# Four-column convolutions with six terms, the first one's terms made by TensorE, and new operation tables for two stages of a two-layer kernel

## The chip, the cores and the metric

The kernel runs on one core of one Trainium2 chip, in one launch. The metric is the device time in microseconds (us). The core has a matrix engine (TensorE, PE in the profile, with its weight loads as PEld), a vector engine (VectorE, DVE), a scalar engine (ScalarE, ACT), GpSimd (POOL) and SyncE (SP), which here only issues DMAs. Each engine runs its own instructions in the order in which the program lists them; a wait at the head of an engine's queue holds everything behind it.

## The reference

The input `x` is 16 samples x 128 channels x 32 x 32, all float32. Two layers are applied, each with a mixing part and a feed-forward part, with a residual added after each. Cut to what matters:

```python
# layer 0
x = x + linear_attention(_ln_c(x))        # layer norm over channels, group norm, q/k/v, 4 heads, output projection
t = tokens(x)
t = t + stu(_ln_t(t))                     # long causal convolutions with 16 filters (by transforms), and 3 short taps
x = image(t)
# layer 1
out = conv3x3(_ln_c(x), w1); out = relu(bn1(out))
out = bn2(conv3x3(out, w2)); x = x + relu(out + _ln_c(x))
t = tokens(x)
t = t + routed_experts(_ln_t(t))          # 64 experts, each takes 8 tokens of each sample
return image(t)
```

The two 3x3 convolutions have 128 input and 128 output channels on 32 x 32 images, with a zero border.

## The kernel before, in words

The program is one function with five stages, one after the other.

1. **Attention** (lines 203 to 748). `class Attention` has one method for each operation on one sample: `tokens` transposes the image (8 transposes), `moments`, `variance`, `root` and `scales` make the layer norm's factors, `norm` scales 8 pieces on ACT, then `channels`, `q_`, `k`, the softmaxes, `context`, two folds of the output matrix, `out`, `out_add`, a second norm, and then the transform of the sample by `even` and `odd` (eight residue classes, butterflies on POOL) and the three-tap part (`taps`, line 618, 24 profile records, `taps_add`). The order of the work is written out by hand in the tuple `period`: each entry is an operation and how many samples ahead it runs, up to 6; a loop goes through it once for each sample. The filters' own transform (`filters`) and the mixing of their matrices (`mst`, 16 steps from 16 loads `mi`) and the preparation of weights on POOL (`prepare`) are generators, one step of which is taken per round. Inputs `x0` and `x1` are loaded first, then `wf`, `phi`; `load(b + 2)` stands in `tokens`. PSUM holds three tiles of 1024 columns (`big`).
2. **Transform convolution** (lines 749 to 846): 16 chunks; `generate` makes the matrices of a chunk on TensorE (L776), ACT and DVE copy them out (L785, L783), `multiply` applies them (L796). The change does not touch it.
3. **Layer 1** (lines 847 to 1352). `class Routed` again has a method for each operation on one sample: the inverse transform (`inverse`, L1039, 16 matmuls), the layer norm (`tokens`, `stats`, `copy`, `root`, `scales` on POOL, `norm`), the image, both convolutions, a second norm and the routing (`logits` to `pooled_copy`, once for a pair of samples).
 A convolution makes two columns from four terms: `terms` (L920, DVE) makes four differences and sums of neighbouring columns, `products` (L926) multiplies one pair of terms for one half of the image by the three rows of transformed weights: six matmuls of 256 columns in a PSUM tile `pcv`. `shift` (ACT, L1097), `sums` (DVE, L1105 and L1106) and `rows` (DVE, L1115 and L1116) combine the four products into the two columns; `relu` (ACT, L1119) writes the next input. So there are 2 x 2 x 12 = 48 matmuls for a sample; the profile has two records for a matmul (L926 x1536).
 The order comes from `planned(table, buffers, ...)`: a list scheduler at build time, with the cost, the due time, the dependences and the tiles of each operation in `table`, which plays the operations through and returns a fixed order. The number after the cost is only a priority.
4. **Experts** (lines 1353 to 1448): 32 weight blocks of 1 MB pass through a ring of nine tiles (`RING`, `load_half`).
5. **Output** (lines 1449 to the end of the function): gates times expert outputs, added to `x` and stored.

The lines of `products` that the change replaces say most:

```python
for i, k in enumerate(ks):
    for dy in range(3):
        nc.tensor.matmul(pc[:, i], wt[:, dy, k, :], v[:, k, hf*HR+dy : hf*HR+dy+HR],
                         start=(dy == 0), stop=(dy == 2))
```

Of the kernel before, what the change touches and what calls it, by code (L numbers as in the profile page):

```python
# [1 line left out]

# [12 lines left out]
P = 128  # L15
B, C, H, W = 16, 128, 32, 32
N = H * W
# [40 lines left out]
HP = H + 2  # L58
WP = W // 2 + 1
HR = H // 2  # L60
WT = W // 2
# [5 lines left out]
def metaformer_kernel(ctx: ExitStack, tc: tile.TileContext, io: dict, out: bass.AP):  # L67
# [96 lines left out]
    with ExitStack() as l0:  # L164
# [7 lines left out]
        cwd = [dram.tile([P, 3, 4, C], F32, name=f"cwd{n}", tag=f"cwd{n}") for n in range(2)]  # L172
# [32 lines left out]
        ph = lconst.tile([P, NCH, CW], F32, name="ph")  # L205


        with ExitStack() as a0:
# [96 lines left out]
            for b in range(2):  # L305
                load(b)
            wqk = aconst.tile([P, 2 * C], F32, name="wqk")
# [16 lines left out]
            nc.vector.tensor_scalar(mu[:, 0], mu[:, 0], wmix[:, 0:1], None, ALU.mult)  # L324
            for i in range(1, NF):
                nc.vector.scalar_tensor_tensor(
                    mu[:, i], mu[:, i], wmix[:, i : i + 1], mu[:, i - 1], ALU.mult, ALU.add
                )

# [11 lines left out]
            class Attention:  # L341
# [10 lines left out]
                def tokens(self):  # L352
                    if self.b + 2 < B:
                        load(self.b + 2)
                    self.x = xt[self.b]
                    self.pt = big().rearrange("p (j c) -> p j c", c=C)
                    transpose_in(self.pt, self.x)
# [34 lines left out]
                def norm(self):  # L392
                    normalize(self.tok, self.tok, self.sts[:, 0], self.sts[:, 3])
# [19 lines left out]
                def q_(self):  # L413

                    self.pq = big()
                    for hf in range(2):
                        cs = slice(hf * HALF, (hf + 1) * HALF)
                        nc.tensor.matmul(
                            self.pq[:, cs], wqk[:, 0:C], self.xn[:, cs], start=True, stop=True
                        )  # L420
# [10 lines left out]
                def k(self):  # L431
# [69 lines left out]
                def fold2(self):  # L501
# [4 lines left out]
                def fold2_copy(self):  # L506
# [39 lines left out]
                def norm2(self):  # L546
                    normalize(self.ub, self.ub, self.sts2[:, 0], self.sts2[:, 3])
# [64 lines left out]
                def taps(self):  # L612

                    self.pa = big()
                    for si, (lo, hi) in enumerate(SEGS):
                        for tap in range(KU):
                            a = max(lo, tap)
                            nc.tensor.matmul(  # L618
                                self.pa[:, a:hi], mu[:, NF - 1 - si, tap, :],
                                self.u[:, a - tap : hi - tap],  # L620
                                start=(tap == 0), stop=(tap == KU - 1),
                            )
# [5 lines left out]
            def filters():  # L628

                wfm = setup.tile([P, NQ // 2, 2 * P], F32, name="wfm", tag="mi")  # L630
                nc.vector.tensor_scalar(wfm, wf[:, 1::2, :], -1.0, None, ALU.mult)

                def values(q, dst):
                    for sgn in range(2):
                        w = wfm[:, q // 2, :] if sgn and q % 2 else wf[:, q, :]
# [4 lines left out]
                yield  # L640
                xf = spectrum_tile()
                for parity in range(2):
                    pe = class_values(parity, values)
                    t = class_copy(pe, 1)
                    ts = class_copy(pe, ROT) if parity else t
                    ab = class_sums(parity, pe, t)
                    class_differences(parity, ab, pe, ts)
                    yield
                    for part in range(2):
                        butterflies(ab, xf, parity, part)  # L650
                    if parity:
                        butterflies(ab, xf, 1, butterflies(ab, xf, 1, 2))
                    yield
                half = CW // 2
                e, o = (xf[:, :, i].rearrange("p c r m j -> p c (r m j)") for i in range(2))
                nc.vector.tensor_tensor(ph[:, :, :half], e, o, ALU.add)
                nc.vector.tensor_tensor(ph[:, :, half:], e, o, ALU.subtract)
                for m in range(EPR // MB):
                    es = slice(m * MB, (m + 1) * MB)
                    for i in range(NF):  # L660
                        mi = setup.tile([P, MB, C], F32, name="mi", tag="mi")
                        nc.sync.dma_start(mi, io["M_phi"][i, :, es, :])
                        yield
                        if i == 0:
                            nc.vector.tensor_scalar(mst[:, es, :], mi, coef[:, 0:1], None, ALU.mult)
                        else:
                            nc.vector.scalar_tensor_tensor(
                                mst[:, es, :], mi, coef[:, i : i + 1], mst[:, es, :], ALU.mult, ALU.add
                            )

            def prepare():
# [4 lines left out]
                for n in range(2):  # L676
# [8 lines left out]
                    eng.tensor_tensor(cw[:, :, 1], raw[:, :, 0], raw[:, :, 2], ALU.add)  # L685
                    yield
                    eng.tensor_tensor(cw[:, :, 2], cw[:, :, 1], raw[:, :, 1], ALU.subtract)
                    yield
                    eng.tensor_tensor(cw[:, :, 1], cw[:, :, 1], raw[:, :, 1], ALU.add)
                    yield  # L690
                    for k, r in ((0, 0), (3, 2)):
                        nc.sync.dma_start(cwd[n][:, :, k], raw[:, :, r])
                    eng.tensor_scalar(cw[:, :, 1:3], cw[:, :, 1:3], 0.5, None, ALU.mult)
                    nc.sync.dma_start(cwd[n][:, :, 1:3], cw[:, :, 1:3])
# [13 lines left out]
            nc.sync.dma_start(wf, io["wf"])  # L708
            phi = spool.tile([P, NQ, 2, P], F32, name="phi", tag="xf")
            nc.sync.dma_start(phi, io["phi"])  # L710


            period = (
                ("q_max", 3), ("out_add", 1), ("tokens", 6), ("moments", 6), ("context", 2),
                ("channels", 4), ("input", 1), ("norm2", 0), ("context_mask", 2),
                ("group_root", 4), ("k_exp", 3), ("fold", 2), ("group_scale", 4), ("moments2", 1),
                ("q_exp", 3), ("even", 0), ("tokens_copy", 6), ("taps_in", 0), ("input_copy", 1),
                ("channels_copy", 4), ("filters", 0), ("fold_copy", 2), ("even_copy", 0),
                ("even_sums", 0), ("taps_copy", 0), ("odd", 0), ("even_turns", 0),
                ("variance2", 1), ("root2", 1), ("q_tokens", 3), ("scales", 5), ("fold2", 2),  # L720
                ("q_copy", 3), ("k_sum", 3), ("scales2", 1), ("root", 6), ("spread", 5),
                ("k_recip", 3), ("k", 4), ("even_turns2", 0), ("q_recip", 3), ("variance", 6),
                ("fold2_copy", 2), ("odd_copy", 0), ("taps", 0), ("odd_sums", 0), ("k_max", 4),
# [877 lines left out]
```

## Time and profile before

| what | value |
|---|---|
| median of 3 runs (lowest, highest) | 1327.79 us (1319.41, 1328.11) |
| the profiled execution's own time | 1324.0 us |
| its span, first to last instruction | 1322.2 us |
| mean granted TensorE clock | 0.971 |
| busy: PE, DVE, ACT, POOL | 92%, 69%, 53%, 38% of the span |
| attention: first instruction to the first L776 | 0 to 395.7 us |
| transform convolution: to the end of the last store's sums | 395.7 to about 686 us |
| layer 1: to the first matmul of the experts | 686 to 1217.5 us |
| experts: to the first L1461 | 1217.5 to about 1293 us |
| output | to 1322.2 us |

How to read it. A group's line has the engine, the operation, its output and inputs with shapes, the count, then busy time and the mean duration of one, and after the second bar the idle time of its engine just ahead of it with what ended it. Neighbouring instructions overlap, so the distance from one start to the next in the timeline is the better price of a matmul or a vector operation in a row of such. A table by windows has, for each stretch, the busy time and number of instructions of each engine, the granted clock and the DMA share. DVE works through its queue in order, as all engines do, so its operations are also a list of when things come free.

### The profile page before, as it was taken

To read this page: it belongs to the slowest core of one execution; us is meant where nothing else is said; L and a number is where in the kernel's file an instruction comes from. 1 tells how busy PE (TensorE), PEld (TensorE's weight loads), DVE (VectorE), ACT (ScalarE), POOL (GpSimd) and SP (SyncE) were. 2 spreads that over 40 slices of the span, in tenths; PEclk is the share of its full clock that TensorE was granted. 3 is DMA by queue.
4 is the path that set the end of the run, shared out by engine and by line. 5 is a ranking of instruction groups with operands and counts; after the bars stand their busy time and mean duration, and the time that the engine had idled before them with its cause. 6 is when DMAs were issued, how large, how long until landed. Compare 5 with 4: busy or idle time off the path is not lost. (4 is left out here: it accounts for less than half of the span.)

```text
span 1322.2 us, 33734 instructions
## 1 busy us (share of the span) xinstructions
PE 1216.7 (92%) x14116; PEld 990.8 (75%) x14116; DVE 907.2 (69%) x1982; ACT 705.2 (53%) x1424; POOL 503.3 (38%) x816
## 2 busy tenths in 40 slices
PE   4889999999998999999956999999999999996886
PEld 3777777777767888888846987989888888883443
DVE  5688887877765666776637767777778676772224
ACT  3777777777545666666623435545555454544111
POOL 2324545454685777777743111222212121110002
PEclk8899999999998999999987999999999999997998
DMA  7014343433344333333367211313122113007986
GB/s 268 17 35 140 118 134 112 144 124 121 114 149 145 127 125 127 127 121 119 107 235 182 70 48 49 88 27 111 32 80 64 33 49 127 17 24 260 374 329 255
DMA packets 87401, 162.99 MB, mean 123 GB/s; under 512 B 5584, under 2 KB 40784, under 8 KB 86864
## 3 DMA queue, kind: packets, MB, share of 16 engines
q1 hardware_dynamic: 86608, 158.33, 36.2%
q8 instruction: 111, 1.82, 0.6%
q0 software_dynamic: 640, 2.49, 0.5%
q14 instruction: 42, 0.34, 0.1%
HBM read 104.18 MB, written 56.62 MB: 122 GB/s over the span
## 5 line engine op out<-in xcount | busy, mean ns | idle before, releaser
L926 PE MATMUL pcv<-v,cw 128*128 128x256 f32 x1536 | 342.9, 380 | 0.0
L926 PEld LDWEIGHTS pcv<-v,cw 128*128 128x128 f32 x1536 | 286.8, 190 | 42.2 <-issue 5.7
L785 ACT COPY g<-pg 128x512 f32<-128x512 f32 x288 | 153.1, 591 | 102.8 <-PE pg L776 102.8
L783 DVE COPY g<-pg 128x512 f32<-128x512 f32 x224 | 145.8, 687 | 90.1 <-PE pg L776 90.1
L776 PE MATMUL pg<-ph,mst 32*128 32x128 f32 x4096 | 155.3, 287 | 4.5 <-ACT g L785 3.0
L776 PEld LDWEIGHTS pg<-ph,mst 32*128 32x128 f32 x4096 | 130.7, 190 | 30.8 <-issue 25.9
L796 PE MATMUL py<-g,v 128*32 128x128 f32 x4096 | 140.1, 276 | 3.8 <-POOL v L768 1.2
L796 PEld LDWEIGHTS py<-g,v 128*32 128x32 f32 x4096 | 105.3, 110 | 20.7 <-issue 2.4
L767 POOL TENSOR_TENSOR v<-xc 128x256 f32<-128x256 f32 x128 | 91.6, 741 | 71.6 <-PE py L796 62.5
L141 ACT ACTIVATE tok<-tok,sts 128x128 f32<-128x128 f32 x256 | 101.8, 481 | 23.8 <-POOL sts L1001 20.4
L132 DVE BATCH_NORM_STATS2 bst<-big 128x6 f32<-128x256 f32 x256 | 91.1, 417 | 19.5 <-PE big L154 12.1
L1066 POOL TENSOR_SCALAR sts<-bst 128x8 f32<-128x8 f32 x16 | 6.5, 406 | 235.7 <-DVE bst L132 235.7
L920 DVE TENSOR_TENSOR v<-pads 128x544 f32<-128x544 f32 x128 | 85.0, 723 | 9.9 <-ACT pads L1119 9.5
L618 PE MATMUL big<-u,mu 128*128 128x128 f32 (+4 forms) x384 | 86.0, 380 | 0.0
L274 POOL TENSOR_TENSOR xf<-ab 128x256 f32<-128x256 f32 x34 | 24.8, 730 | 132.0 <-DVE ab L241 131.9
L618 PEld LDWEIGHTS big<-u,mu 128*128 128x128 f32 x384 | 56.7, 191 | 18.0 <-issue 15.4
L1097 ACT ACTIVATE ct<-pcv,bn 128x256 f32<-128x256 f32 x64 | 30.3, 474 | 68.8 <-PE pcv L926 67.9
L551 PE MATMUL big<-wf,ub 128*128 128x256 f32 x256 | 62.0, 385 | 0.2
L149 PEld LDWEIGHTS big<-ident,x 128*128 128x128 f32 x384 | 47.3, 148 | 19.2 <-issue 7.2
L149 PE MATMUL big<-ident,x 128*128 128x128 f32 x384 | 53.6, 286 | 8.5 <-DVE x L1048 3.4
L1115 DVE TENSOR_TENSOR r<-pcv,cs 128x256 f32<-128x256 f32 x64 | 26.9, 420 | 49.0 <-PE pcv L926 48.2
L141 ACT ACTIVATE tt<-tt,sts 128x128 f32<-128x128 f32 x128 | 51.1, 480 | 9.2 <-POOL sts L1001 8.9
(231 smaller groups left out, 2271.3 us busy)
## 6 DMA issues: line engine op xcount, KB each, us to landing
we<-in_weight SPq DMA_DIRECT2D x32, 1024.0 KB, 9.7
vd<-xf SPq DMA_DIRECT2D x16, 1024.0 KB, 5.1
xc<-vd SPq DMA_DIRECT2D x64, 256.0 KB, 3.5
yd<-ys SPq DMA_DIRECT2D x32, 512.0 KB, 3.8
y<-yd SPq DMA_DIRECT2D x15, 896.0 KB, 6.5
x<-in_x SPq DMA_DIRECT2D x16, 512.0 KB, 4.1
mi<-in_M_phi SPq DMA_DIRECT2D x16, 512.0 KB, 4.9
xd<-x SPq DMA_DIRECT2D x16, 512.0 KB, 6.0
```

The lines of the kernel that those rows point to most:

```text
L132: nc.vector.bn_stats(bst[:, j : j + 2, :].rearrange("p j s -> p (j s)"), src[:, j : j + 2, :].rearrange("p j c -> p c j"),)
L141: nc.scalar.activation(dst[:, j, :], src[:, j, :], AF.Identity, bias=nm[:, j : j + 1], scale=r[:, j : j + 1],)
L149: nc.tensor.transpose(pt[:, j, :], src[:, j * P : (j + 1) * P], ident)
L551: nc.tensor.matmul(dst, self.ub[:, q, :], wf[:, q, :], start=True, stop=True)
L618: nc.tensor.matmul(self.pa[:, a:hi], mu[:, NF - 1 - si, tap, :], self.u[:, a - tap : hi - tap], start=(tap == 0), stop=(tap == KU - 1),)
L767: nc.gpsimd.tensor_tensor(vv[:, x, 1:, bs], e, o, op)
L776: nc.tensor.matmul(pg[r][:, i], mst[rs, 4 * q + i, :], ph[rs, c, :], start=True, stop=True,)
L783: nc.vector.tensor_copy(dst, src)
L785: nc.scalar.copy(dst, src)
L796: nc.tensor.matmul(py[rows, x, kl, :], v[:, (x * NM + m) * JL + jl, 1 - ri : 3 - ri, :] .rearrange("p k b -> p (k b)"), g[:, ((x * 2 + ri) ...
L920: nc.vector.tensor_tensor(v[:, k], d[i], d[j], op)
L926: nc.tensor.matmul(pc[:, i], wt[:, dy, k, :], v[:, k, hf * HR + dy : hf * HR + dy + HR], start=(dy == 0), stop=(dy == 2),)
```

## The change

It does these things.

- **Convolutions.** Four columns are made from six terms (a one-dimensional minimal filtering over columns with 4 outputs and 3 taps). The image is kept as 4 residues of columns x 32 rows x 8 groups, so a term has 256 columns for the whole image. `products` now takes two terms and the whole image: 6 matmuls, two of 256 columns and four of 248 (the border rows are left out, so no zero rows are kept). There are three such calls in a convolution (`inside`, `next`, `outer`), 36 matmuls for a sample's two.
- **First convolution's terms.** For it, TensorE makes the six terms from the normed tokens: `terms(i)` has 4 matmuls with a constant matrix `bt` of 192 columns, twice; ACT copies them out (`terms_copy`). The image itself is still made, for the residual.
- **Second convolution's terms** are made on DVE from the padded output of the first (`inside_terms`, `next_terms`, `outer_terms`: three instructions of 576 elements and six of 256). The products are combined by `inside_copy`, `next_copy` (ACT), `inside_sums`, `columns`, and `edges_a` or `rest` (DVE). The first batch norm's shift moves into `relu`'s bias, the second's into `rest`.
- **Transformed weights**: 6 instead of 4 sets, made by more steps of `prepare` on POOL and stored and loaded with 9 KB per partition for each convolution.
- **Attention's order** comes from `planned` too, with a table of costs and due times; `norm` and `taps` are cut into two operations, the steps of the filters and of `prepare` are operations of their own. All inputs `x0` to `x7` are asked for at the start, behind `wf` and `phi`; the first weights to be prepared come after them.
- **Layer 1's table** is new. The planner takes tiles in turn. At the start of the stage SP loads `x0`, then `y0`, `wi`, then `x1`, `y1`, then the conv weights; before, `wi` and the conv weights came first, and GpSimd issued `x0` and most of `y0`. The memset of the padded image has 1152 elements instead of 3468.
- **Small moves**: tiles of the weight ring, `b1`, `ot` and the last stage's `yt`.

```diff
-        def products(v, wt, hf, ks):
-            pc = ps.tile([P, 2, HR, WT], F32, name="pcv", tag="cv", bufs=3)
+        def products(v, wt, ks):
+            pc = ps.tile([P, 2, IMG], F32, name="pcv", tag="cv", bufs=3)
             for i, k in enumerate(ks):
-                for dy in range(3):
+                for dy in (1, 0, 2):
+                    lo, hi = max(0, 1 - dy), min(H, H + 1 - dy)
                     nc.tensor.matmul(
-                        pc[:, i], wt[:, dy, k, :], v[:, k, hf * HR + dy : hf * HR + dy + HR],
-                        start=(dy == 0), stop=(dy == 2),
+                        pc[:, i, lo * GT : hi * GT], wt[:, dy, k, :],
+                        v[:, k, lo + dy - 1 : hi + dy - 1].rearrange("p h g -> p (h g)"),
+                        start=(dy == 1), stop=(dy == 2),
                     )
+            def terms(self, i):
+                pv = self.pv[i] = big().rearrange("p (j w) -> p j w", j=4)
+                for j in range(4):
+                    nc.tensor.matmul(
+                        pv[:, j, : NTERM * 4 * GT], self.tok[:, 4 * i + j], bt, start=True, stop=True
+                    )
+            def terms_copy(self, i):
+                if i == 0:
+                    self.v = term_tile()
+                rows = slice(i * H // 2, (i + 1) * H // 2)
+                nc.scalar.copy(
+                    self.v[:, :, rows].rearrange("p t (j r) g -> p t j (r g)", j=4),
+                    self.pv[i][:, :, : NTERM * 4 * GT].rearrange("p j (t w) -> p t j w", t=NTERM),
+                )
+            def inside_terms(self):
...
+                nc.vector.scalar_tensor_tensor(
+                    zt[:, 0:2], columns(2, 1), -4.0, columns(4, 3), ALU.mult, ALU.add
+                )
+                a, b = rows(zt[:, 0]), rows(zt[:, 1])
+                nc.vector.tensor_tensor(v[:, 1], a, b, ALU.add)
+                nc.vector.tensor_tensor(v[:, 2], a, b, ALU.subtract)
...
+            def inside_sums(self):
+                sd = self.sd = work.tile([P, 2, IMG], F32, name="cs", tag="cs")
+                m = self.pc[1, 2][:, 0]
+                nc.vector.tensor_tensor(sd[:, 0], m, self.cti, ALU.add)
+                nc.vector.tensor_tensor(sd[:, 1], m, self.cti, ALU.subtract)
+            def columns(self):
...
+                nc.vector.scalar_tensor_tensor(nd[:, 0], self.ctn, 0.5, m, ALU.mult, ALU.add)
+                nc.vector.scalar_tensor_tensor(nd[:, 1], m, 2.0, self.ctn, ALU.mult, ALU.subtract)
+                self.r = [work.tile([P, 2, IMG], F32, name="r", tag="r") for _ in range(2)]
+                nc.vector.tensor_tensor(self.r[0], nd, self.sd, ALU.add)
+                nc.vector.scalar_tensor_tensor(self.r[1], nd, 4.0, self.sd, ALU.mult, ALU.add)
+            def rest(self, i):
+                self.edge(i)
+                r, os = self.r[i], slice(2 * i, 2 * i + 2)
+                nc.vector.scalar_tensor_tensor(
+                    r, r, bn[:, 1, 1:2], self.p1[:, os].rearrange("p o h k -> p o (h k)"),
+                    ALU.add, ALU.add,
+                )
+                xs = self.x.rearrange("p (n o) -> p o n", o=4)[:, os]
+                nc.vector.scalar_tensor_tensor(xs, r, 0.0, xs, ALU.max, ALU.add)
...
-            period = (
-                ("q_max", 3), ("out_add", 1), ("tokens", 6), ("moments", 6), ("context", 2),
...
+            table = (
+                ("tokens", "PE", 0.88, -286.5, "", "big:X x", ""),
+                ("moments", "DVE", 1.38, -253.7, "tokens", "", "big:X"),
...
+                ("f_matrix", "DVE", 1.4, 82.7, "", "", ""),
+                ("prepare", "POOL", 2.4, -52, "", "", ""),
             )
...
+            ("terms 0", "PE", 0.68, -277.6, "norm1", "big:v0", ""),
+            ("terms 1", "PE", 0.68, -196.6, "terms0", "big:v1", "tok"),
+            ("terms_copy 0", "ACT", 0.84, -263.1, "terms0", "v:a", "big:v0"),
+            ("terms_copy 1", "ACT", 0.84, -244, "terms1 terms_copy0", "", "big:v1"),
+            ("inside_a", "PE", 2.55, -142, "terms_copy1", "cv:a12", "v:a"),
```

## The prediction

> **What bounds the kernel now.** First the page, for the share of each engine; then the table by windows, one row for each stage and one for the steady middle of layer 1.
>
> ```profile
> PE 1216.7 (92%) x14116; PEld 990.8 (75%) x14116; DVE 907.2 (69%) x1982; ACT 705.2 (53%) x1424; POOL 503.3 (38%) x816
> L926 PE MATMUL pcv<-v,cw 128*128 128x256 f32 x1536 | 342.9, 380 | 0.0
> ```
>
> ```profile
> 0.00:395.70 395.70, 359.36 (x2052) 281.84 (x2052) 299.05 (x739) 261.70 (x539) 185.76 (x299) 0.98 0.38 123
> 686.00:1217.50 531.50, 498.73 (x2952) 434.35 (x2952) 383.47 (x824) 255.75 (x513) 102.61 (x256) 0.97 0.26 78
> 1217.50:1293.00 75.50, 61.62 (x856) 29.54 (x856) 20.02 (x50) 9.56 (x16) 0.00 (x0) 0.99 0.89 334
> 760.00:1090.00 330.00, 328.24 (x1977) 288.31 (x1976) 253.61 (x550) 168.85 (x339) 70.03 (x169) 1.00 0.21 58
> 0.00:20.00 20.00, 8.17 (x28) 6.85 (x29) 10.02 (x54) 6.17 (x12) 4.99 (x12) 1.00 0.84 319
> 20.00:40.00 20.00, 13.64 (x49) 10.95 (x49) 9.35 (x30) 10.53 (x28) 4.04 (x8) 0.66 0.33 124
> 60.00:80.00 20.00, 15.76 (x102) 12.32 (x103) 18.30 (x54) 16.14 (x35) 4.45 (x3) 1.00 0.00 1
> ```
>
> (Columns: stretch, length, busy PE, PEld, DVE, ACT, POOL, granted clock, DMA share, GB/s.) From 760 to 1090 us, eleven samples of layer 1 (88 of its 128 norms on `tok`), PE is busy 328.2 of 330 us, and the table of waits has one PE wait there, of 1.7 us. So a sample costs its PE work, 30.0 us, and only less PE work shortens it. DVE has 23.05 us a sample, ACT 15.35. Layer 1 is 531.5 us though 16 x 30 is 480: 51 us go at its start and end. The experts run at DMA share 0.89 and gain nothing. In attention PE is not full at the start: rows 1, 2 and the last.
>
> The price of a matmul is the distance of starts in the timeline of PE:
>
> ```profile
> 908.10 5.35 PE L926 MATMUL pcv<-v,cw 128*128 128x256 f32 x24
> 913.28 0.61 PE L1039 MATMUL big<-wi,y 128*128 128x128 f32 x4
> 913.73 1.50 PE L1039 MATMUL big<-wi,z 128*128 128x128 f32 x12
> 915.07 0.61 PE L1039 MATMUL big<-wi,y 128*128 128x128 f32 x4
> 915.51 1.50 PE L1039 MATMUL big<-wi,z 128*128 128x128 f32 x12
> 916.85 2.76 PE L926 MATMUL pcv<-v,cw 128*128 128x256 f32 x12
> 919.44 1.04 PE L149 MATMUL big<-ident,x 128*128 128x128 f32 x8
> ```
>
> 12 matmuls of 256 columns take 913.28 - 908.10 = 5.18 us, 0.432 each (two records each); 16 of 128 columns take 3.57, 0.223 each. The line through both, 0.014 + 0.001633 N, gives 0.419 for 248 columns and 0.328 for 192.
>
> **What the skill says.** The Trainium skill, "FP8 and Floating Point Precision", TensorE Precision Notes: true FP32 is four passes through the array. An estimate from this with the warm 2.4 GHz of "TensorE: Matmul & The Clock Gate", What's actually happening, is 256 x 4 / 2.4 = 427 ns; the trace has 432. So cost follows columns, and fewer columns are the only way. The same section says that the array runs at half clock until it has been busy some 3.4 us; the trace agrees in kind (0.66 in the row 20 to 40, where PE has gaps). "VectorE: DVE Perf Modes", The TRN2 errata: an fp32 tensor_tensor of N elements takes (N + 151)/0.96 ns; 691 ns at 512, and the trace has 694 (L1145). It gives 757 for 576.
>
> **Layer 1, PE.** Removed for each sample: 48 x 0.432 = 20.74. Added: 12 x 0.432 + 24 x 0.419 = 15.24, and `terms`, 8 x 0.328 = 2.62. Saved 20.74 - 17.86 = 2.88. My sum of a sample's PE before (inverse 3.57, four times eight transposes 3.52, convolutions 20.74, half of a pair's routing 2.3) is 30.1, against 30.0 seen; after, 27.25. Sixteen samples: **-46**. (The table's entry for four `terms` matmuls is 0.68; I keep 1.31. If 0.68 were right, another -20.)
>
> **Layer 1, DVE and ACT.** DVE removed: `terms` 8 x 0.66 (start to start) = 5.3, `sums` 3.3, `rows` 3.3, the end of `rest` 2.8: 14.7. Added: 12 operations of 256 at 0.413, 8 of 512 at 0.693, 3 of 576 at 0.76, 6 sums at 0.414: 15.3. DVE becomes 23.05 + 0.6 = 23.6 of 27.25, 87%. ACT loses the shifts (4 x 0.474 = 1.9), gains four copies of 256 (0.386 each, row L822) and two `terms_copy` of 768, about 0.80 each between L822 and the 1.01 of a copy of 1024: some 16.6. Neither is the bound by sum, if strides cost nothing: the new operands step by 9 or 4 elements. The trace shows one such price: L1048, which writes with stride 8, takes 1222 ns for 1024 elements, and L449, in order, 1217. From below zero, from above half rate (rival D).
>
> **Layer 1, waits.** I laid the changed order of each queue out with these prices over a pair of samples. The tightest chain is `outer` products, `edges_a` (0.8), two `relu` (1.2, behind a `copy` on ACT at worst 1.0), `inside_terms` (1.45), then `inside_b`: 4.3 to 4.8 us. PE has tokens 0.88 + inverse 3.57 = 4.45 between in one sample of a pair, and 6.2 in the other. So up to 0.5 us a pair of stall, 54.6 us + 0.5 for two: **+6** over the stage with the `terms_copy` wait, which the image (0.88) covers. PSUM: `big` is used eight times a sample, not six, for about 22 of 2 x 27 tile-microseconds: no wait by sum.
>
> **Layer 1, start and end.** Before, the first convolution starts at 723.75, behind the DVE `terms` (2.6) and a memset of the padded image (2.99). The terms come from PE and the memset is a third: -4 to -6. SP's order works against it: `x0`, a `yd` store, `y0`, then `wi` (asked for at 671 before), and the conv weights, 2.4 MB, behind `x1` and `y1`: +1 to 2. `y` of the last sample is late as before (stored 684, landed 694.7). At the end the last sample has 2.9 us of cover for the 4.3 to 4.8 chain, and `rest` after the last product is 3.5 where `rows` and its sequel was about 2: +3. Start and end: 0. Layer 1: -46 + 6 = **-40**, range -20 to -50.
>
> **Attention.** PE content is the same, about 336 us at 20.8 a sample. In steady work the period is 21.88 us (first `taps` at 94.84, next 116.73, then 138.61), so about 1 us a sample is lost, and at 94.84 PE had done 54 us worth at full clock: 40 lost before that. The change pulls other work into these gaps (the mixing steps, 16 x 1.27 us of DVE; filters) but all of it needs DVE, which has 18.3 of 20 busy from 60 to 80. In the new order the fifth `taps_add` stands behind 150 us of DVE work, which begins at 9.7; at 85 to 95% DVE that is 168 to 186, centre 176, and PE content up to there is 142.5 as in the old one at 187.6: **-11**, later -1. Against it: GpSimd's `k_scale` and `f_odd_turns` now stand behind a burst of `prepare` (about 1 us for each 384 columns) that waits for raw weights asked for behind eight inputs; and SP's `mi` loads stand behind stores that wait for that burst. If PE waits there for 10 to 15 us the gain is gone. Range -28 to +5, taken **-12**.
>
> The rest (the transform stage, nine ring tiles as before, experts, output): 0, since the transform stage's instructions are the same and the experts are at 334 GB/s.
>
> **Sum.** 1322.2 - 40 - 12 = 1270 span; the profiled time is 1.8 above its span, so 1272. That execution, 1324.0, stands 3.8 below the median, 1327.79, and within the runs' spread of 8.7.
>
> **Rivals.**
> A. DVE's order binds: at 87%, an in-order DVE makes PE wait 1.4 us a sample (28.7 instead of 27.25). For: two new chains PE-DVE-ACT-DVE-PE a sample; against: before, at 77%, it cost nothing. Layer 1 -22, total 1290. Chance 0.2.
> B. Attention gives nothing, since DVE is its bound early, or the `prepare` burst takes what is gained; layer 1 as forecast: 1284. Chance 0.17.
> C. `terms` is as cheap as the table says, or attention fills its whole gap: 1250. Chance 0.1.
> D. The other side: strided DVE operands at half rate. The strided ones would take their elements' time once more at 0.96 per ns (three of 576 0.60 each, six of 256 0.27, the four of 512 in `rest` 0.53): 5.5 us, DVE 29.1, and with the waits of a full in-order engine a period of 31.7. Layer 1 +26, nothing from attention: 1350. It decides from about +3.6 us of DVE a sample, where DVE passes 27.25; L1048 speaks against it. Chance 0.06.
>
> **How the numbers follow.** The forecast, -40 and -12, has 0.47; its own range is 1258 to 1285. Leaving out D and the ends of A and C, 1243 to 1308 holds 8 in 10. About 1% (13 us) is what a measurement of this kernel can tell from no change: faster takes the forecast, B, C and most of A, 0.87; within 1%, A's end with B together, 0.06; slower D and a little more, 0.07.
>
> **What would show it.** L926's line falls from 1536 records to 1152, mean near 375 ns, with 256 records of 192 columns on a new line near 0.33 us start to start. In the middle of layer 1 eleven samples take 300 us with PE above 97% busy (A: 316 and PE waits for `v` or for DVE; D: 340 with 576-element operations above 1.2 us). Layer 1 then is near 490 us. In attention the first L776 comes near 384 (B: 395 or later, with PE waits on POOL names in the first 100 us). I am wrong in the whole if the steady sample is over 29 us, or if a wait for `wi` or the conv weights of over 5 us stands at the head of layer 1.

## The result and the profile after

The changed kernel takes 1334.63 us in the median of 13 runs (1328.46 to 1340.04), against 1324.39 us (13 runs) for the kernel before: the ratio is 1.0086, interval 1.0066 to 1.0106. It is a little slower, by 0.9% with an interval that stays clear of 1, where -52 us was forecast. The profiled execution has a span of 1334.4 us.

The page of the changed kernel, the two lines that answer to those shown of before:

```profile
PE 1199.6 (90%) x13988; PEld 973.5 (73%) x13988; DVE 950.2 (71%) x1998; ACT 725.0 (54%) x1456; POOL 519.4 (39%) x828
L1059 PE MATMUL pcv<-v,cw 128*128 128x248 f32 (+1 forms) x1152 | 256.7, 376 | 4.0 <-DVE v L1265 2.5
```

The convolutions cost what was worked out: 1152 records, mean 376 ns, and 86 us less of PE than before; `terms` take 47 of them (256 records of 192 columns). Yet PE as a whole is busy not 39 but 17 us less, and DVE 43 us more, where 10 were forecast. The table by windows of the changed kernel (columns as before) says where:

```profile
0.00:426.40 426.40, 374.99 (x2056) 293.18 (x2056) 311.71 (x739) 264.09 (x539) 206.10 (x314) 0.94 0.36 118
716.70:1221.70 505.00, 460.34 (x2827) 406.67 (x2827) 413.80 (x840) 273.08 (x545) 101.82 (x256) 0.95 0.28 86
1221.70:1305.10 83.40, 68.15 (x858) 30.62 (x858) 20.07 (x50) 9.55 (x16) 0.00 (x0) 0.91 0.85 309
800.00:1100.00 300.00, 296.83 (x1880) 266.12 (x1878) 275.27 (x557) 179.50 (x363) 71.36 (x176) 1.00 0.21 61
```

| stage | before | after | difference | forecast |
|---|---|---|---|---|
| attention | 395.7 | 426.4 | +30.7 | -12 |
| transform convolution | 290.3 | 290.3 | 0 | 0 |
| layer 1 | 531.5 | 505.0 | -26.5 | -40 |
| experts | 75.5 | 83.4 | +7.9 | 0 |
| output | 29.2 | 29.3 | +0.1 | 0 |
| span | 1322.2 | 1334.4 | +12.2 | -52 |

(The end of the transform convolution is taken as 290.3 us behind the end of attention in both. Its last sums end 288.5 and 288.8 us behind it, so the stage is the same.)

So two questions are open: what attention lost, and why layer 1 with the experts behind it gained 18.6 instead of 40.

**Attention.** The table of waits of PE in this stage of the changed kernel (line waited for, us in all, times, longest) begins with:

```profile
PE pc L495 <- POOL ke L474: 12.1, 3, 6.0
```

Two of the three are in PE's timeline at 65 and 82 us, in front of `context`, which needs `ke` from GpSimd:

```profile
64.72 0.42 PE L397 MATMUL pg<-gt,avg 128*128 128x1 f32 x2
71.06 3.79 PE L495 MATMUL pc<-ke,qt 128*128 128x128 f32 x16 [5.92 <-POOL ke L474]
...
80.05 1.88 PE L527 MATMUL big<-xn,wt 128*128 128x512 f32 x4
87.89 3.78 PE L495 MATMUL pc<-ke,qt 128*128 128x128 f32 x16 [5.95 <-POOL ke L474]
```

The timeline of GpSimd shows what stood ahead of `k_scale` (L474) in its queue, all of it weight preparation:

```profile
64.67 1.17 POOL L736 TENSOR_SCALAR pcw<-raw 128x384 f32<-128x384 f32 x1
65.93 1.00 POOL L738 TENSOR_TENSOR pcw<-pcw,raw 128x384 f32<-128x384 f32 x1
66.89 1.17 POOL L740 TENSOR_SCALAR raw<-raw 128x384 f32<-128x384 f32 x1
68.14 0.99 POOL L742 TENSOR_TENSOR pcw<-pcw,raw 128x384 f32<-128x384 f32 x1
69.09 1.91 POOL L474 TENSOR_TENSOR ke<-ke,ks 128x1024 f32<-128x1024 f32 x1
...
82.90 3.05 POOL L759 TENSOR_SCALAR pwi<-pwi,seg 128x128 f32<-128x128 f32 x3 [7.48 <-DMA pwi<-in_wi]
85.92 1.92 POOL L474 TENSOR_TENSOR ke<-ke,ks 128x1024 f32<-128x1024 f32 x1
```

DVE's reciprocals that release the two `k_scale` end at 58.6 and 66.5 us. They run at 69.1 and 85.9, so 10.5 and 19.4 us late: the first behind the arithmetic, the second also behind a preparation step that waits for a load (`pwi`), which SP could issue only at 77.1, after a store that waits for that same arithmetic. PE's direct wait is the smaller part, and the engines pass it on, since each works in order: DVE stands 8.4 and 8.0 us for the `context` that PE has not made, and PE, with gaps of several us, loses its clock, 0.70 and 0.73 from 60 to 100 us. Two rows of the table by windows for the changed kernel, and the stretch from 20 to 120 us before and after:

```profile
60.00:80.00 20.00, 12.39 (x57) 9.87 (x56) 10.44 (x29) 8.05 (x17) 14.85 (x12) 0.70 0.27 87
80.00:100.00 20.00, 10.91 (x47) 8.75 (x46) 10.84 (x41) 10.46 (x28) 7.96 (x7) 0.73 0.28 105
20.00:120.00 100.00, 85.11 (x497) 69.23 (x497) 74.53 (x204) 69.12 (x143) 33.84 (x47) 0.91 0.22 72
20.00:120.00 100.00, 70.22 (x335) 55.70 (x334) 67.22 (x148) 50.77 (x108) 66.06 (x74) 0.81 0.35 119
```

 GpSimd is busy 66 us there for 34. Busy time of PE times granted clock, summed over the rows of 20 us up to 120, is 87 us before and 68 after (an estimate from the table by windows): 19 us of array work are missing there, and 11 more by 200 us. From 200 to 380 the new order is the better one, PE full, first `taps` at 256.06, 277.07, 298.13: 21.0 us a sample for 21.9.

### The profile page after: what moved, and what is told of

It is laid out like the page before. It is cut to its first block, busy times and chain, and to the rows that moved or that the text cites. A ratio compares the mean times of both kernels' runs of the same rounds, so it can differ in the third digit from the quotient of the medians.

```text
span 1334.4 us, 33591 instructions
## 1 busy us (share of the span) xinstructions
PE 1199.6 (90%) x13988; PEld 973.5 (73%) x13988; DVE 950.2 (71%) x1998; ACT 725.0 (54%) x1456; POOL 519.4 (39%) x828
## 5 line engine op out<-in xcount | busy, mean ns | idle before, releaser
L1059 PE MATMUL pcv<-v,cw 128*128 128x248 f32 (+1 forms) x1152 | 256.7, 376 | 4.0 <-DVE v L1265 2.5
L1059 PEld LDWEIGHTS pcv<-v,cw 128*128 128x128 f32 x1152 | 214.2, 190 | 30.8 <-DVE v L1265 4.7
L903 PE MATMUL pg<-ph,mst 32*128 32x128 f32 x4096 | 152.5, 284 | 4.8 <-ACT g L912 3.4
L903 PEld LDWEIGHTS pg<-ph,mst 32*128 32x128 f32 x4096 | 128.2, 187 | 30.9 <-issue 24.8
L141 ACT ACTIVATE tok<-tok,sts 128x128 f32<-128x128 f32 x256 | 103.6, 481 | 29.9 <-POOL sts L1150 21.3
L1221 POOL TENSOR_SCALAR sts<-bst 128x8 f32<-128x8 f32 x16 | 8.9, 556 | 164.3 <-DVE bst L132 164.3
L1395 POOL TENSOR_SCALAR sts<-bst 128x8 f32<-128x8 f32 x16 | 6.2, 389 | 169.1 <-DVE bst L132 169.1
L474 POOL TENSOR_TENSOR ke<-ke,ks 128x1024 f32<-128x1024 f32 x16 | 30.9, 1931 | 101.4 <-DVE gt L391 68.0
L149 PE MATMUL big<-ident,x 128*128 128x128 f32 x384 | 52.9, 283 | 13.4 <-DVE x L1381 7.6
L149 PEld LDWEIGHTS big<-ident,x 128*128 128x128 f32 x384 | 45.0, 146 | 19.0 <-issue 9.6
L1292 ACT ACTIVATE ct<-pcv 128x256 f32<-128x256 f32 x64 | 24.1, 378 | 60.8 <-PE pcv L1059 57.6
```

Of the source, the lines that this page charges most:

```text
L141: nc.scalar.activation(dst[:, j, :], src[:, j, :], AF.Identity, bias=nm[:, j : j + 1], scale=r[:, j : j + 1],)
L149: nc.tensor.transpose(pt[:, j, :], src[:, j * P : (j + 1) * P], ident)
L903: nc.tensor.matmul(pg[r][:, i], mst[rs, 4 * q + i, :], ph[rs, c, :], start=True, stop=True,)
L1059: nc.tensor.matmul(pc[:, i, lo * GT : hi * GT], wt[:, dy, k, :], v[:, k, lo + dy - 1 : hi + dy - 1].rearrange("p h g -> p (h g)"), start=( ...
```

## Experiments

The parts of layer 1 in the table: head (to the first product), middle (to the last), tail (to the first matmul of the experts). The transform stage counts as 290.3 us in every run; where it is shorter, the head is shorter by as much. Ratios are to the kernel before, with their intervals. Stage times come from one profile each; stages that a run does not touch repeat within some 4 us (attention), 10 us (the heads), 2 us (the middle) and 0.1 us (the tail).

| run | ratio | attention | head, middle, tail | experts |
|---|---|---|---|---|
| before | 1 | 395.7 | 37.6, 463.5, 30.3 | 75.6 |
| after | 1.0086 (1.0066 to 1.0106) | 426.4 | 33.3, 435.9, 35.8 | 83.4 |
| old_attention | 0.9816 (0.9778 to 0.9854) | 393.5 | 27.8, 437.5, 35.8 | 84.2 |
| late_prepare | 0.9842 (0.9797 to 0.9886) | 394.8 | 32.6, 435.8, 35.8 | 84.3 |
| late_mixing | 1.0112 (1.0080 to 1.0144) | 424.2 | 38.1, 437.5, 35.8 | 84.9 |
| early_burst | 0.9961 (0.9941 to 0.9981) | 415.0 | 29.4, 437.5, 35.8 | 84.3 |
| spread_both | 0.9897 (0.9866 to 0.9929) | 401.7 | 32.8, 435.9, 35.7 | 84.8 |
| late_both | 0.9895 (0.9828 to 0.9961) | 405.2 | 30.9, 435.8, 35.8 | 84.4 |
| warm_tail | 1.0067 (1.0047 to 1.0086) | 422.3 | 31.3, 435.9, 35.8 | 84.5 |
| warm_full | 0.9758 (0.9722 to 0.9794) | 392.5 | 29.9, 437.4, 32.8 | 79.5 |
| contiguous_rest | 0.9768 (0.9729 to 0.9808) | 393.0 | 30.6, 433.8, 33.3 | 83.2 |
| rest_pairs | 0.9700 (0.9667 to 0.9733) | 392.8 | 31.2, 433.6, 30.9 | 78.4 |
| rows_last | 0.9762 (0.9730 to 0.9795) | 392.4 | 30.8, 435.9, 32.9 | 77.5 |
| before_warm | 0.9968 (0.9951 to 0.9985) | 395.4 | 38.4, 463.5, 29.0 | 76.2 |

### Which part loses: the old order of attention under the new layer 1

**old_attention**: the loop through `period` of the kernel before, its loads, and the steps of preparation one or two per round. The core of the edit:

```diff
-                for b, name in planned(
-                    table, buffers, B, 102.38, left_out, ready
-                ):
...
+                for p in range(-reach, B):
+                    for _ in range(1 + (p >= 0)):
+                        next(preparing, None)
+                    for name, d in period:
...
```

> The changed kernel with the attention stage in the old written-out order, its loads as before, and two steps of the weight preparation per round from the ninth on. Theory (the new order of attention loses the time, the new layer 1 gains it): attention ends near 396 us instead of 426, layer 1 keeps its 505, so the whole is near 1304 us, ratio to the kernel before 0.984. Rival (the larger preparation, 36 steps for 22, is what costs, whatever the order): attention ends above 410 and the ratio is above 0.995.

Attention ends at 393.5, the ratio is 0.982: the new layer 1 and the larger preparation are a gain by themselves, and the loss belongs to the new order of attention, with its loads and its placing of the preparation.

### Preparation or mixing: one line each

**late_prepare** and **late_mixing** each change one line in `ready`, the time from which the planner may place such steps.

```diff
                 if name == "f_matrix":
-                    return 25.0 + 6.0 * b
+                    return 150.0 + 10.0 * b     (late_mixing)
                 if name == "prepare":
-                    return 22.0 + 3.0 * b
+                    return 150.0 + 12.0 * b     (late_prepare)
```

> The changed kernel with one number of the planner's input changed: the steps of the weight preparation may start from 150 + 12 b us instead of 22 + 3 b. Theory (k_scale and the filter's turns stand on GpSimd behind the preparation's burst, PE waits, its clock falls): the waits of PE for ke disappear, attention ends at or below 396, ratio 0.985 or lower. Rival (DVE is full, or the mixing steps wait for their loads): attention still ends above 415, ratio above 1.0.

> The changed kernel with the mixing steps of the filter matrices allowed from 150 + 10 b us instead of 25 + 6 b; the preparation stays early. Theory of the GpSimd burst: PE still waits 10 us or more for ke, attention ends above 415, ratio above 1.0. Rival (the mixing steps' DVE work and the loads behind SP's stores delay the start): attention ends below 405, ratio below 0.995.

With the preparation late, PE's waits for `ke` are gone and attention ends at 394.8: 31.6 us come back with one line. With the mixing late they stay at 12.1 us and attention at 424.2. The theory of the burst holds, its rival falls.

**early_burst** is the reverse: the good old order (old_attention) gets the burst.

```diff
-                    for _ in range(1 + (p >= 0)):
+                    for _ in range(7):
                         next(preparing, None)
```

> The kernel with the old attention order and the new layer 1 (old_attention, ratio 0.982), with one change: seven steps of the weight preparation per round from the first round on, so that all 36 run in the first six rounds as they do early in the changed kernel. Theory (a burst of preparation ahead of k_scale and the filter's turns on GpSimd costs the time): attention ends at 400 to 425 us instead of 393.5, ratio 0.987 to 1.005. Rival (the burst is harmless and the new order's other choices cost it): attention ends below 397, ratio 0.98 to 0.985.

It does what the theory says: PE waits 13.2 us for `ke`, the first `taps` move from 92.6 to 114.1 us, and attention ends 21.5 us later. So the burst is shown as cause from both sides, by taking it out and by putting it in. How much of the 31 us comes by the waits for `ke`, and how much by the other work behind the burst (the filter's turns on GpSimd, the loads behind SP's stores), was not separated.

### Why the new order gains nothing even then

In late_prepare the first `taps` stand at 82.8 us, 12 us earlier than before, as the prediction had it; but attention ends where it did. The 12 us overstate the lead: busy time of PE times clock, summed as above, is 6 us ahead of the kernel before at 120 us (93 for 87), 5 at 160, and level at 200 us. So the lead is lost between 160 and 200. The row of 150 to 200 us in the table by windows of late_prepare:

```profile
150.00:200.00 50.00, 44.10 (x254) 35.15 (x254) 46.61 (x93) 33.57 (x71) 31.43 (x41) 0.97 0.44 141
```

DVE is 93% busy there and PE waits. Two runs tried to place the filler elsewhere: **spread_both** (preparation from 60 + 20 b, mixing from 30 + 18 b) and **late_both** (180 + 12 b and 150 + 12 b), with edits in the same two lines.

> The changed kernel with both kinds of background work spread over the stage: preparation allowed from 60 + 20 b us, mixing steps from 30 + 18 b. Theory (in late_prepare the first taps came 12 us earlier than before, at 82.8 us, and the 12 were lost again between 140 and 200 us, where DVE is 94% busy with mixing steps): spread out, attention ends at 382 to 390 and the ratio is 0.972 to 0.98. Rival (the new order cannot hold the lead, since DVE and PSUM limit its steady work): attention ends at 393 or later, ratio 0.983 or more.

> The changed kernel with preparation from 180 + 12 b us and mixing steps from 150 + 12 b, both behind the start. Theory (the new order does bring the first taps 12 us forward, and the mixing steps that are then packed where DVE is full give them back): with the mixing behind the first 150 us and at 12 us each, attention ends at 384 to 390, ratio 0.974 to 0.980. Rival (no place is free: DVE is near its bound, so the 20 us of mixing cost what they save wherever they go): attention ends at 393 or later, ratio 0.983 or more, as in late_prepare (394.8) and spread_both (401.7).

Both times the rival was right: 401.7 and 405.2. Each new number gives a quite different order: in these two the first `taps` stand at 96.3 and 95.5 us, so they did not even have the early start that they were to keep, and they do not test what took it in late_prepare. What can be said is where DVE's time goes: in late_prepare it is busy 319 us up to 395 us with the same 739 instructions that took 298 before. The groups that grew are the smallest: the operations on `ga` (128x1), 64 of them, from 10.6 to 23.4 us, most of the rest being those on 128x8. Their single records are long when GpSimd is at work: of the 48 that work on `ga` alone, 45 have no GpSimd instruction beside them in the kernel before and take 0.16 us in the mean; in late_prepare 38 have one, and take 0.44. The timeline of DVE in the changed kernel, and below it that of GpSimd:

```profile
104.86 0.31 DVE L124 TENSOR_TENSOR ga<-ga 128x1 f32<-128x1 f32 x1
105.20 0.66 DVE L125 SCALAR_TENSOR_TENSOR ga<-ga 128x1 f32<-128x1 f32 x1
105.90 0.38 DVE L126 SCALAR_TENSOR_TENSOR ga<-ga 128x1 f32<-128x1 f32 x1
```

```profile
104.42 0.72 POOL L285 TENSOR_TENSOR xf<-ab 128x256 f32<-128x256 f32 x1 [13.57 <-DVE ab L252]
105.11 0.73 POOL L287 TENSOR_TENSOR xf<-ab 128x256 f32<-128x256 f32 x1
105.81 1.69 POOL L291 TENSOR_TENSOR xf<-ab 128x128 f32<-128x128 f32 x4
```

L125 takes 0.66 us for one element per partition, and ends at 105.86 when GpSimd's L287 does; without such a neighbour it takes 0.16. The Trainium skill, "SBUF — State Buffer", SBUF: two separate sides, says that DVE with two SBUF inputs and GpSimd take a shared port pair for a whole instruction and the other blocks; the records agree with that. Whether it is this stretching, the place of the mixing or PSUM that eats the lead was not separated; it stays open.

### The experts: a cold array

In the changed kernel the first blocks of the experts run at half clock. PE's timeline:

```profile
1221.68 1.94 PE L1615 MATMUL ph<-we,pooled 128*32 128x512 f32 x8 [0.38 <-DVE pooled L1491]
1223.55 1.93 PE L1622 MATMUL ph<-b,ident 64*32 64x512 f32 x8
```

In the kernel before:

```profile
1217.55 1.07 PE L1374 MATMUL ph<-we,pooled 128*32 128x512 f32 x8 [0.38 <-DVE pooled L1257]
```

In all nine profiles of the new layer 1 other than warm_full, rest_pairs and rows_last below, the longest single record of these matmuls takes 1.06 us, for 0.62 in the one profile of the kernel before. The granted clock is 0.50 from 1221.7 to 1229.2 and 0.66 up to 1239.2, and the next loads of the ring wait for tiles that these blocks hold: SP issues the third of them 11.4 us after the first matmul of the experts, for 6.7 before. Two runs put matmuls with unused output into the gaps of PE behind the last sample; `warm(n)` makes n products of `ident` with itself, of 128 columns.

```diff
+                if b == B - 1 and name == "tokens2":
+                    warm(12)     (warm_full alone)
                 perform(samples[b], name)
...
+                elif b == B - 1 and name == "tokens2":
+                    warm(15)     (10 in warm_tail)
                 elif b == B - 1 and name == "logits":
+                    warm(34)     (16 in warm_tail)
```

> The changed kernel with 10 idle transposes-worth matmuls (128 columns, output unused) after the last sample's second transposes and 16 after the last logits, in gaps where PE waits 5.5 and 8 us. Theory (the experts start with a cold array, clock 0.91, which frees the ring's tiles late): from the last convolution to the end 148 us becomes 138 to 142, ratio 1.002. Rival (the experts are late through the loads alone): 146 to 150, ratio 1.008.

> old_attention with 12, 15 and 34 matmuls of 128 columns whose output is not used, in the three gaps of PE after the last convolution, so that no gap is over about 1.5 us. Theory (a cold array at the start of the experts costs some 6 us and the tail before it some 4): the experts take 76 to 79 us instead of 84.2, ratio to the kernel before 0.973 to 0.977. Rival (the loads alone set the experts): 83 to 85 us, ratio 0.98 to 0.983.

warm_tail (on the changed kernel) changed neither the tail nor the experts, so its expectation failed: its 16 matmuls end at 1203.3 and PE then stands 4.3 us, after which the clock is at half again. With the gaps filled (warm_full, on old_attention) PE's timeline of the same place reads:

```profile
1177.63 1.07 PE L149 MATMUL big<-ident,gt 128*128 128x128 f32 x8 [0.27 <-DVE gt L1511]
1179.80 1.97 PE L1533 MATMUL pp<-tt,gtt 128*64 128x128 f32 x32 [1.10 <-ACT gtt L1526]
1182.90 1.06 PE L1683 MATMUL ph<-we,pooled 128*32 128x512 f32 x8 [0.38 <-DVE pooled L1548]
```

Turn, pool and hidden layer run at full clock (1.07, 1.97, 1.06 for 1.94, 3.68, 1.94), the third load of the ring comes 6.7 us after the first matmul again, the tail falls by 3.0 and the experts by 4.7, to 79.5, half a microsecond above what was expected. The Trainium skill, "TensorE: Matmul & The Clock Gate", What's actually happening, gives some 3.4 us of idling or of work as what turns the clock. Here the array is cold after the gap of 4.3 us in warm_tail, and warm after the gaps of at most 1.1 us behind the 34 matmuls in warm_full. But in warm_full it is also cold, at half clock from 1162.5 to 1169.3, after a gap of only 2.1 us (to 1161.75) with eight transposes spread over 3.2 us behind it; the matmuls of the logits bring it back, and the 34 hold it. So a gap shorter than 3.4 us was not enough to keep it warm there. The experts are at 77.5 to 79.5 with it, in three runs, still 2 to 4 us above 75.6; that rest stays open. The control, **before_warm**, puts the last 34 into the kernel before:

```diff
                 elif b == B - 1 and name == "logits":
+                    pt = big()
+                    for _ in range(34):
+                        nc.tensor.matmul(pt[:, :P], ident, ident, start=True, stop=True)
```

> The kernel before with 34 unused matmuls of 128 columns after its last logits. Theory (its experts start warm already, at clock 1.00; only the last turn and pool run cold): the tail of layer 1 falls by 2 to 3 us, the experts stay at 75.6, ratio 0.997 to 0.999. Rival (the kernel before has the same loss hidden elsewhere): the experts fall too, ratio 0.995 or lower.

The kernel before has nothing to win in the experts (76.2 for 75.6), since they start warm; its tail gains 1.3, less than expected. Why its array is warm again 7.5 us after the gap of 8 us (half clock until 1217.0, half a microsecond ahead of the experts), and that of the changed kernel only 22 us after it (at 1235.9), with the same work in the first 8 us, is open.

### Layer 1: is it DVE?

In the steady part the samples of the changed kernel follow each other as forecast: the image additions of two pairs stand at 931.55 and 987.33, so 27.89 us a sample; before, 952.97 and 1013.65, so 30.34. The additions after, then before:

```profile
931.55 1.21 DVE L1203 TENSOR_TENSOR x<-big,x 128x1024 f32<-128x1024 f32 x1
987.33 1.21 DVE L1203 TENSOR_TENSOR x<-big,x 128x1024 f32<-128x1024 f32 x1
952.97 1.22 DVE L1048 TENSOR_TENSOR x<-big,x 128x1024 f32<-128x1024 f32 x1
1013.65 1.22 DVE L1048 TENSOR_TENSOR x<-big,x 128x1024 f32<-128x1024 f32 x1
```

That is -2.45, and 16 of them -39, for -46 + 6 in the prediction. But DVE has 25.9 us of the 27.9, where 23.6 was forecast. The groups of DVE in layer 1 of the changed kernel:

```profile
L1381 DVE SCALAR_TENSOR_TENSOR x<-r,x 128x512 f32<-128x512 f32 x32 | 35.8, 1120 | 1.1
L1376 DVE SCALAR_TENSOR_TENSOR r<-r,bn,pads 128x512 f32<-128x512 f32 x32 | 24.1, 752 | 1.1
L1270 DVE TENSOR_TENSOR zt<-pads 128x576 f32<-128x576 f32 x16 | 15.1, 945 | 0.0
```

L1381 reads and writes `x` in steps of four elements and takes 1120 ns for a forecast of 693. L1270 takes 740 ns in ten records and about 1280 in six; the one at 983.45 us overlaps the `z` sums of GpSimd at 983.24 (L1107, L1108), as with `ga` above. All six long records lie beside these sums of 256 elements, and none of the ten short ones does. Two runs change L1381 alone, contiguous_rest on old_attention and rest_pairs on warm_full. contiguous_rest leaves out the order of the columns: it adds to other columns of `x` than the layer asks for, so its output is not the layer's. It has the same operations on the same shapes, and only its time is used.

```diff
-                xs = self.x.rearrange("p (n o) -> p o n", o=4)[:, os]
+                xs = self.x.rearrange("p (o n) -> p o n", o=4)[:, os]     (contiguous_rest)
-                nc.vector.scalar_tensor_tensor(xs, r, 0.0, xs, ALU.max, ALU.add)     (rest_pairs)
+                xs = self.x.rearrange("p (n o) -> p n o", o=4)[:, :, os]     (rest_pairs)
+                rn = r.rearrange("p o n -> p n o")     (rest_pairs)
+                nc.vector.scalar_tensor_tensor(xs, rn, 0.0, xs, ALU.max, ALU.add)     (rest_pairs)
```

> old_attention where the last addition of the second convolution goes to contiguous halves of x instead of columns in steps of four (it leaves the order of columns wrong, and the work the same). Theory (layer 1 in the steady part is bound by PE; the strided addition, 1.11 us for 0.69, is hidden): the addition falls to 0.69, layer 1 gains 0 to 2 us, at its end, ratio 0.980 to 0.983. Rival (DVE binds): 0.84 us a sample, layer 1 gains 10 to 14, ratio 0.972 to 0.975.

> warm_full (ratio 0.976) with the last addition to x walking pairs of neighbouring columns (x in runs of two elements, r in steps of 256) instead of one column at a time in steps of four elements; the result is the same. Theory (the 1.11 us come from single elements of x at a pitch of four): the addition falls to 0.7 to 0.8, the middle of layer 1 from 437.4 to 434 and its tail from 32.8 to about 31, ratio 0.971 to 0.974. Rival (any strided operand costs it): 1.1 us or more, ratio 0.976 or above.

The addition falls to 692 and to 704 ns; this is its group in rest_pairs:

```profile
L1439 DVE SCALAR_TENSOR_TENSOR x<-r,x 128x512 f32<-128x512 f32 x32 | 22.5, 704 | 1.1
```

The ratio of contiguous_rest, 0.977, lies between the two expectations, and neither is right; its stages tell more. Both times the middle loses 3.7 to 3.8 us and the tail 1.9 to 2.5. A bound by DVE would have given 0.84 x 16 = 13 us. The steady pair of samples takes 55.78 us in rest_pairs (image additions at 894.32 and 950.10) as in the changed kernel, so DVE is not the bound there. The gain comes from the first and the last samples, where the addition is not hidden: it stands between the last product and the second norm's transposes, and PE's waits for it (L149 for the `x` of this line in old_attention, 3.7 us in the middle) fall to 1.2 in rest_pairs. As expected of the pitch, a run of two elements of `x` is enough, while `r` in steps of 256 costs nothing that can be seen. The Trainium skill, "SBUF — State Buffer", Door 1: The DMA port swizzle, states lines of 16 bytes in SBUF, full speed for at least two accesses to a line, and a penalty for each new line; single floats at a pitch of four have one per line (1120 ns), pairs two (704), which agrees for `x`. But `r` in steps of 256 also has one access per line, and shows no such cost, so the rule as stated does not cover all of it; `x` is both read and written here, and which of the two costs was not tried. rest_pairs is the fastest kernel of the study, 1286.98 us in the median, 0.970 of the kernel before.

**rows_last** asks whether the tail is longer because `rest` now works by columns:

```diff
+                if self.b == B - 1:
+                    for hf in range(2 if i else 0):
+                        for k in range(2):
...
+                            xs = self.x[:, hf * N // 2 : (hf + 1) * N // 2]
+                            xs = xs.rearrange("p (n o) -> p o n", o=4)[:, os]
```

> warm_full with the last sample's rest in halves of the image, so that its first four transposes need only the first half. Theory (with columns in steps of four, the second norm's transposes wait for all of rest, where the kernel before let four of them go after half): the tail of layer 1 falls from 32.8 by 0.5 to 1.5 us. Rival (ACT's copy and the statistics set the tail): no change of the tail, or a rise by the four added instructions' fixed time, some 0.5.

The tail is 32.9 for 32.8: this guess of mine is wrong. Four transposes do start early, at 1153.2, but the last of the additions, now in halves, ends 5.4 us after the start of the last product for 5.0, and the tail is no shorter.

## Why the prediction was wrong, step by step

- **Attention, -12: wrong in sign, and the largest error (43 us).** The step that failed reads "If PE waits there for 10 to 15 us the gain is gone. Range -28 to +5". The wait was named in its place, and its size was right (12.1 us). What failed was to price a wait by its own length, with +5 as the end: the stage with this wait in it came out at +30.7, and 31.6 came back when the burst behind it went. I laid out DVE's queue against its work and took DVE at 85 to 95%; it was at 67% from 20 to 120 us, since it waited for PE, which waited for GpSimd. The prediction saw that `k_scale` stands behind the burst, but GpSimd's queue was not laid out in time: then `k_scale` 10 and 19 us late would have been seen, and SP's store ahead of the load that GpSimd waits for. late_prepare (-31.6) and early_burst (+21.5) show the cause.
- **The lead at the start** (11 us) came in late_prepare alone, as 12 us at the first `taps` but some 6 us of PE's work; that it lasts was wrong, and attention ends 11 to 21 us late in three placings (394.8, 401.7 and 405.2 for 384). Where the rest went stays open.
- **Layer 1, PE and waits, -46 + 6 = -40:** right in the sum, -39, but in part by luck. The wait forecast at +6 is hardly there, 0.06 us of idle time of PE a sample, and PE's own saving is smaller by about as much, by small stalls that do not show as idle: 27.83 us busy a sample for 27.25 (the distance from the logits' matmuls to the next is 2.12 us for 1.87 before). The sample before was 30.34, not 30.0: the 330 us hold 10.9 samples, not eleven.
- **Layer 1, start and end, 0:** this term was +12.5 (-26.5 less -39): the tail +5.5, against a head of -4.3, and nearly 12 in the first and last samples of the middle, whose 463.5 fell by 27.6 and not by 39. PE idles 9 us in the middle for 2 before, all of it ahead of 817 us or behind 1140; the other 4 to 5 are not accounted for. With the array warm and the addition by pairs (rest_pairs) layer 1 is at 495.7, -35.8.
- **Experts, 0:** failed. "the experts are at 334 GB/s" is an average; the first blocks hold the ring, and at half clock they release it late. It cost 7.9, of which warm_full gave 4.7 back.
- **Rival D** (strided operands at half rate) was right for one operation of those named: the two `rest` additions to `x` cost 0.43 each more, 0.86 a sample, under the 3.6 at which it would decide. With what stretches beside GpSimd, DVE came to 25.9 for 23.6. My evidence against it was misread: L1048 walks `x` in order, and its strided operand is the one in PSUM. (L1145, set beside the skill's price of a tensor_tensor, is a scalar_tensor_tensor; a tensor_tensor of 512, L1306, takes 697 ns.) **Rival A** does not hold: steady period 27.89. **Rival B** came nearest, though it stopped at 1284: attention's loss was not bounded at zero.

## What to carry to other kernels

When work is moved forward to fill idle time, lay out the queue of the engine that gets it, with what is ready when behind it, and the DMA queue with its stores; a background step belongs behind the first critical operations, not ahead. Price a wait in the start of a pipeline by what the in-order engines behind it lose, clock included, not by the wait: here PE's 12 us of waiting stood in a stage that grew by 31 us. A stage that moves data at full rate can still be set by its first blocks.

## What of the hardware was not expected

- DVE operations on one element per partition stretch from 0.16 to between 0.3 and 0.7 us beside GpSimd arithmetic, and a 576-element one from 0.74 to 1.28.
- A DVE operation on single floats at a pitch of four takes 1120 ns for 512 elements, on pairs 704, contiguous 692.
- Matmuls without a use, put into idle gaps of at most 8 us, took some 7 us off a kernel of 1300 by the array's clock (1299.0 for old_attention, 1292.29 for warm_full; the two stages say 7.7).
